# Window scores of all heads in one run and one exponential, split loads of rows, and weights one item later, in an attention and convolution kernel

## The chip, the cores and the metric

The kernel runs on one core of one Trainium2 chip. The metric is the device time of one execution in microseconds (us), as the median of the runs shown. Five engines of the core work side by side, each through its own list of instructions: TensorE (PE, with its weight loads shown as PEld), VectorE (DVE), ScalarE (ACT), GpSimd (POOL) and SyncE (SP), which here only issues transfers. Transfers (DMAs) are issued by SP, ACT or POOL and carried out by 16 shared DMA engines.

## What is computed

The input x has 2 images of 256 channels and 64 x 64 pixels. Two layers follow one another, both in fp32:

```python
# layer 0
q, k, v = 1x1 convolutions of x            # 8 heads of 32 channels, all 4096 pixels
fuse    = softmax(q k^T / sqrt(32)) v
x       = conv1x1(concat(x, fuse)) * m + x * (1 - m)     # m: mask, 32x32 resized to 64x64
# layer 1
x = x * sigmoid(relu(x ca_w1 + ca_b1) ca_w2 + ca_b2)     # gate per pixel and channel
o = softmax(q k^T / 8) v                   # in windows of 8x8 pixels, 4 heads of 64 channels
x = x + o out_w + out_b
x = shuffle(x)                             # channels in 4 groups
y = relu(bn(conv7x7(x, 64 groups)))        # 256 -> 64 channels
y = bn(conv7x7(y, 64 groups))              # 64 -> 256 channels
out = x * sigmoid(y)
```

## The kernel before

**Prologue** (to about 178 us). The 1x1 projections of the 16 chunks (image b, 512 pixels c) are computed (`L450`, `L489`) and stored to DRAM. The copy of v out of PSUM goes through tiles of the tag "v" of a pool with two buffers (`L500`, `L501`); the last chunk's copy is shared by ACT and DVE.

**Attention of layer 0.** For each image b, chunk c, group g of four heads and block m of 128 keys there is a *slot*, 1024 in all. In a slot, `scores` (`L666`) multiplies keys and queries of a block two slots ahead, ACT takes the exponentials (`L679`), `products` (`L718`) multiplies them by v, and DVE adds up the exponentials in two alternating sums (`L724`). In the last chunk there is one sum only (`chains = 1`), so each addition waits for the one before. Denominators (`dn`, `L752`), their reciprocal (`L779`) and the division of the attention result f (`L785`) come some slots later, by a list of due times (`at`). Actions are delayed by a number of slots.

**The stage of a chunk.** `stage(b, c)` (`L789`) is a generator that does the rest of layer 0 and the windows of layer 1 for a finished chunk, while PE goes on with the slots of the next one. One step, up to a `yield`, runs every fourth slot. It computes the mix (hy), the gate (ca1, ca2, tanh), u (`L861`), q and k of the windows in two halves of the heads (`project`, `project_out`), scores, softmax, v, the transposed probabilities (pt, `L980`, `L988`), their product with v (o, `L999`), the output projection (op) and the sum xo = y + u (`L1032`), which is stored to `x_s` in DRAM (`L1047`), padded for the convolutions. The window softmax is done for each half of the heads `hc` separately: 32 matmuls (`L905`), one copy to SBUF (`L913`), one maximum on DVE (`L917`), eight exponentials on ACT with the maximum as bias and the sum as accumulated output (`L926`), then reciprocal and product on DVE (`L937`, `L938`). The stage is put on the list by `at(DN + 8 + late, ...)`; `late` is 5 for most chunks, 13 for the first and 0 for the last two.

**The convolutions.** `convolve()` is a second generator, for the tail. Channels are cut in 16 units u of four input groups. There are 26 *items*: 0 to 8 are units 0 to 8 of image 0, 9 to 15 units 2 to 8 of image 1, 16 to 21 units 9 to 14 with both images (*pair items*), then unit 15 of each image, and units 1 and 0 of image 1. Item k takes its rows from `x_s` (420 KB an image; `load_rows`, `load_x`, on SP), its banded weights from `w_s` (896 KB a unit; `load_w`, `L1088`, on SP), does the first convolution (c1, `L1177`; of pair items `L1144`, which works with differences of columns, `dx`, `L1116`, and sums of weights, `both`, `L1121`, both on DVE), the second (c2, `L1203`), tanh and copy on ACT (`L1214`, `L1220`), the product with x on DVE (`gate`, `L1230`) and 12 or 24 stores of the output (`store`, `L1257`) on several queues. The order within the loop is c1 of item k+1, with `both` of item k+2 behind it, then c2 of k, gate of k, loads of rows, stores of k, and the next weight tile:

```python
conv1(k + 1)
z = conv2(k)
gate(k, z)
load_rows(...)
store(k, z)
if weights and (weights[0] <= 1 + EB or k >= EARLY + 4):
    load_w(weights.popleft())
```

`weights` holds the units 1 to 15 and 1 again; EB is 8 and EARLY is 9. Units 0 to 6 are loaded at the start, 7 to 9 after items 1 to 3, and unit 10 after item 13. As each engine works in the order of the program (the kernel schedules by hand), this order is also that of the queues. Items 0 to 8 begin between the last slots and the last stages. Items of image 1 need the last stage's x_s; the list `staged` says that it has been stored, and then `more()` makes the tiles `xcs` for later items and loads the rows of item 9.

Of the kernel before, what the change touches and what calls it, by code (L numbers as in the profile page):

```python
# [10 lines left out]
F32 = mybir.dt.float32  # L11
# [8 lines left out]
P = 128  # L20
# [37 lines left out]
def conv_seq_kernel(ctx: ExitStack, tc: tile.TileContext, a, out):  # L58
# [315 lines left out]
    with (  # L374
# [109 lines left out]
        for i, (b, c) in enumerate(chunks):  # L484
# [14 lines left out]
            for copy, ms in evict:  # L499
                v = st0.tile([P, KC, 4, P], F32, tag="v", name=f"vst_{b}_{c}_{ms.start}")  # L500
# [55 lines left out]
    def pipeline(arm, shifted, pools):  # L556
# [232 lines left out]
        def stage(b, c):  # L789
# [71 lines left out]
            nc.vector.scalar_tensor_tensor(u, t, 1.0, x1, ALU.add, ALU.mult)  # L861
            yield True

            qks, es_, mxs, sums = [], [], [], []

            def project(hc):
                s = psum2(f"qk{tag}_{hc}")
                for j in range(2):
                    o = (KC * j + hc) * P
                    for kc in range(KC):  # L870
# [25 lines left out]
            def window_scores(hc):  # L896
                qk = qks[hc]
                s = psum2(f"sc{tag}_{hc}")
                for t in range(4):
                    for w in range(2):  # L900
                        for h in range(2):
                            r = slice(64 * h, 64 * h + 64)
                            p = 64 * ((w + t) % 2)
                            tok = slice(t * P + 64 * w, t * P + 64 * w + 64)
                            nc.tensor.matmul(  # L905
                                s[p : p + 64, h, 64 * t : 64 * t + 64],
# [5 lines left out]
                e = wp.tile([P, 8, 64], F32, tag=f"ew{hc}", name=f"ew{tag}_{hc}")  # L912
                nc.scalar.copy(  # L913
                    e.rearrange("p (h n) k -> p h (n k)", h=2), s[:, :, 0 : 4 * 64]
                )
                mx = gp.tile([P, 8], F32, tag=f"mxw{hc}", name=f"mxw{tag}_{hc}")
                nc.vector.tensor_reduce(mx, e, AX.X, ALU.max, negate=True)  # L917
                es_.append(e)
                mxs.append(mx)


            def window_exp(hc):
                e, mx = es_[hc], mxs[hc]
                rs = gp.tile([P, 8], F32, tag=f"rsw{hc}", name=f"rsw{tag}_{hc}")
                for n in range(8):
                    nc.scalar.activation(  # L926
                        e[:, n, :],
                        e[:, n, :],
                        AF.Exp,
                        bias=mx[:, n : n + 1],  # L930
                        accum_out=rs[:, n : n + 1],
                    )
                sums.append(rs)

            def normalise(hc):
                e, rs = es_[hc], sums[hc]
                nc.vector.reciprocal(rs, rs)  # L937
                nc.vector.tensor_mul(e, e, rs.unsqueeze(2).to_broadcast([P, 8, 64]))  # L938
# [520 lines left out]
```

## Time and profile before

| | us |
|---|---|
| runs shown | 2892.77, 2894.96, 2895.96 |
| median | 2894.96 |
| profiled execution | 2891.88 |
| its span | 2890.0 |
| mean granted clock of PE, as a share of full speed | 0.997 |

Of the span, the prologue takes about 178 us, the 1024 slots with the stages of 15 chunks about 2500, and the tail, in which the last stage and the convolutions run, about 210. The heaviest groups of instructions:

```profile
L679 ACT ACTIVATE ea<-sa 128x512 f32<-128x512 f32 (+1 forms) x3072 | 2038.8, 745 | 56.4 <-PE sa L666 24.3
L666 PE MATMUL sa<-qa,ka 32*64 32x512 f32 x16384 | 1145.7, 614 | 3.0 <-DVE vst L501 2.9
L718 PE MATMUL ava<-ea,va 128*32 128x512 f32 x8192 | 1092.0, 605 | 0.4
```

A line of a group names source line, engine, operation, output and inputs with shapes and the count; then busy time in us and the mean of one in ns; then idle time of the engine just before, and what ended most of it. In a timeline a line gives start and length in us, the engine ("SPq" is SP issuing a transfer), the line, what is done, how often in a row, and in brackets how long the engine had been idle and what released it. Matmuls overlap, so what counts of PE is the distance from one start to the next.

### The profile page before, as it was taken

Reading aid. Unit: us, or ns where it says so; the run is one execution under the profiler, and the core shown is the slowest. Engines: PE = TensorE matmul, PEld = TensorE weight load, DVE = VectorE, ACT = ScalarE, POOL = GpSimd, SP = SyncE. Lnnn points to the kernel's source line nnn. Section 1 sums busy time; section 2 is a strip of 40 time slices with the busy share of each in tenths; the row PEclk is TensorE's granted clock in tenths of the full one; section 3 lists DMA queues with packets and bytes.
Section 4 is the critical chain, followed back from the end, with each engine's and each line's share of the span. In section 5 each row is a group of like instructions: output and inputs, shape, how many; then the busy total and the mean of one; then the engine's idle time right before and its main releaser. Section 6 shows DMA issues by size and latency. Waiting matters only on the chain.

```text
span 2890.0 us, 85875 instructions
## 1 busy us (share of the span) xinstructions
PE 2860.5 (99%) x37198; PEld 836.0 (29%) x37198; DVE 2452.6 (85%) x1370; ACT 2459.4 (85%) x4151; POOL 571.0 (20%) x939
## 2 busy tenths in 40 slices
PE   9999999999999999999999999999999999999998
PEld 4541122222222222222222222222222222222676
DVE  3349999999999999999999999999999999999323
ACT  5569989898989898998989898989989898989434
POOL 8111111111111212121120111111211110010376
PEclk9999999999999999999999999999999999999999
DMA  8545433333243434343333334333434432142575
GB/s 262 206 162 189 148 88 74 97 80 91 69 102 77 106 76 95 87 99 87 81 92 75 92 71 96 80 91 84 100 83 89 95 81 84 56 123 64 159 203 137
DMA packets 245755, 305.67 MB, mean 106 GB/s; under 512 B 121272, under 2 KB 137836, under 8 KB 245112
## 3 DMA queue, kind: packets, MB, share of 16 engines
q1 hardware_dynamic: 200084, 231.51, 27.7%
q0 software_dynamic: 40496, 65.79, 12.1%
q8 instruction: 294, 4.82, 0.7%
q10 hardware_dynamic: 4788, 2.79, 0.3%
q14 instruction: 93, 0.76, 0.1%
HBM read 221.88 MB, written 66.39 MB: 100 GB/s over the span
## 4 chain that ended last, share of the span: by engine, by line
PE 94%; DMA 2%; issue 1%; DVE 1%; ACT 1%; SPq 1%; POOL 0%; DVEq 0%; POOLq 0%; ACTq 0%
PE sa L666 36%; PE ava L718 34%; PE hya L552 4%; PE qka L552 4%; PE c2a L1203 2%; PE q L450 2%; PE vwa L552 2%; PE opa L552 2%; PE k L450 2%; PE v L489 2%; PE c1a L1177 1%; PE sca L905 1%; PE c1a L1144 1%; PE oa L999 1%; PE pta L980 1%
## 5 line engine op out<-in xcount | busy, mean ns | idle before, releaser
L679 ACT ACTIVATE ea<-sa 128x512 f32<-128x512 f32 (+1 forms) x3072 | 2038.8, 745 | 56.4 <-PE sa L666 24.3
L666 PE MATMUL sa<-qa,ka 32*64 32x512 f32 x16384 | 1145.7, 614 | 3.0 <-DVE vst L501 2.9
L724 DVE TENSOR_TENSOR suma<-suma,ea 128x2048 f32<-128x2048 f32 x480 | 1096.4, 2284 | 6.2 <-ACT ea L679 1.1
L718 PE MATMUL ava<-ea,va 128*32 128x512 f32 x8192 | 1092.0, 605 | 0.4
L724 DVE TENSOR_TENSOR odda<-odda,ea 128x2048 f32<-128x2048 f32 x420 | 958.3, 2282 | 2.4 <-ACT ea L679 0.5
L696 POOL DMA_DIRECT2D folda<-suma x336 | 235.5, 874 | 1618.4 <-DVE suma L726 1510.3
L666 PEld LDWEIGHTS sa<-qa,ka 32*64 32x64 f32 x16384 | 241.4, 130 | 787.3 <-ACT ea L679 716.7
L718 PEld LDWEIGHTS ava<-ea,va 128*32 128x32 f32 x8192 | 161.6, 108 | 834.0 <-issue 805.2
L1257 POOL DMA_DIRECT2D out_dram<-za x212 | 119.7, 573 | 46.1 <-DVE za L1230 25.6
L552 PE MATMUL qka<-ua,qkv_w 128*32 128x512 f32 x1024 | 115.8, 592 | 0.7 <-DVE ua L861 0.7
L1047 POOL DMA_DIRECT2D xs<-xo x94 | 67.2, 722 | 206.5 <-DVE xo L1032 203.0
L808 ACT ACTIVATE ta<-hya,bf 128x512 f32<-128x512 f32 x32 | 20.2, 684 | 95.2 <-PE hya L552 95.2
L724 DVE TENSOR_TENSOR odda<-ea,ea 128x2048 f32<-128x2048 f32 x30 | 68.6, 2288 | 37.3 <-ACT ea L679 37.3
L469 DVE TENSOR_REDUCE top<-sq 128x128 f32<-128x2048 f32 x16 | 36.6, 2286 | 74.5 <-ACT sq L463 74.5
L764 POOL DMA_DIRECT2D invs<-inva x62 | 34.1, 557 | 287.4 <-DVE inva L779 286.4
L1203 PE MATMUL c2a<-yca,wa 32*64 32x192 f32 (+1 forms) x2912 | 85.0, 368 | 2.2 <-issue 2.0
L926 ACT ACTIVATE ewa<-ewa,mxwa 128x64 f32<-128x64 f32 x256 | 85.3, 346 | 1.5 <-DVE mxwa L917 1.5
L724 DVE TENSOR_TENSOR suma<-ea,ea 128x2048 f32<-128x2048 f32 x32 | 73.2, 2287 | 11.5 <-DMA ka<-ks 8.5
L1214 ACT ACTIVATE za<-c2a 128x384 f32<-128x384 f32 x64 | 27.9, 487 | 62.1 <-PE c2a L1203 34.0
L917 DVE TENSOR_REDUCE mxwa<-ewa 128x8 f32<-128x512 f32 x32 | 21.9, 685 | 63.3 <-ACT ewa L913 63.3
L1203 PEld LDWEIGHTS c2a<-yca,wa 32*64 32x64 f32 x2912 | 67.7, 191 | 18.0 <-issue 10.5
L884 ACT ACTIVATE qka<-qka,qkv_b 128x512 f32<-128x512 f32 x64 | 40.2, 680 | 37.9 <-PE qka L552 37.9
(166 smaller groups left out, 1698.6 us busy)
## 6 DMA issues: line engine op xcount, KB each, us to landing
ka<-ks SPq DMA_DIRECT2D x256, 256.0 KB
va<-vs SPq DMA_DIRECT2D x256, 256.0 KB
wa<-ws SPq DMA_DIRECT2D x17, 896.0 KB
ws<-zeros SPq DMA_DIRECT2D x16, 896.0 KB
folda<-suma POOLq DMA_DIRECT2D x224, 64.0 KB, 3.2
folda<-suma POOLq DMA_DIRECT2D x112, 128.0 KB, 3.6
xs<-xo POOLq DMA_DIRECT2D x78, 140.0 KB, 6.1
qs<-qst SPq DMA_DIRECT2D x16, 512.0 KB
```

Of the source, the lines that this page charges most:

```text
L450: nc.tensor.matmul(s[:, g, :], w[:, kc, g * P : (g + 1) * P], rhs, start=(kc == 0), stop=(kc == KC - 1),)
L489: nc.tensor.matmul(sv[:, m, :], xs0[i][:, kc, m * P : (m + 1) * P], wv[:, kc, :], start=(kc == 0), stop=(kc == KC - 1),)
L552: nc.tensor.matmul(out[o : o + 32], weights[:, o : o + 32], x, start=start, stop=stop)
L666: nc.tensor.matmul(heads[j][o], k[r, cols][:, o], q[r, g, :], start=True, stop=not shifted)
L679: nc.scalar.activation(e[:, h, :], tile, AF.Exp, scale=SCALE0)
L696: nc.gpsimd.dma_start(dst[p : p + rows], total[rows * k : rows * k + rows, h, :], accum_op=ALU.add if k else ALU.bypass,)
L718: nc.tensor.matmul(av[r, :], v[:, m % PB, r], e[:, j, :], start=start, stop=stop)
L724: nc.vector.tensor_add(total, first.pop(m % chains, total), e)
L926: nc.scalar.activation(e[:, n, :], e[:, n, :], AF.Exp, bias=mx[:, n : n + 1], accum_out=rs[:, n : n + 1],)
L1047: eng.dma_start(x_s[b, n, p + r0 : p + r1].rearrange("r g w -> g r w"), xo[64 * h : 64 * h + 64, oc, r0 - WS * c : r1 - WS * c, :],)
L1203: nc.tensor.matmul(tiles[j // 2][o, j % 2, 0 : n * W], w[r, d, o], y[r, 0:n, d : d + W], start=(d == 0), stop=(d == KS - 1),)
L1257: eng.dma_start(*args)
```

## The change

The window softmax of a stage is done for all heads at once: both projections, then one run of 64 score matmuls into one PSUM tile, one copy, one maximum, a subtraction on DVE, one exponential of 128x1024 on ACT without bias and without accumulated sum, and sum, reciprocal and product on DVE. A stage has two steps fewer. u is made in two halves and `project` goes over its inputs in the outer loop. The tag "v" gets three buffers. The stage of chunk (1,6) starts four slots later. The last stage stores its x_s in three parts of the channels and, after the first, loads the rows of items 9 to 11. Rows are loaded up to item k+4; while item k has one image, they are loaded in three pieces an image, put between the stores of item k on SP (`queue`). c1 of odd items with one image uses another PSUM tile. Copy and gate of the last two items go by blocks of rows, and their stores and those of the two items before go by other queues. `both` and `yt` use other SBUF tiles. Weight units 10 to 15 and 1 are issued from item 14 on (`EARLY + 5`).

```diff
-                v = st0.tile([P, KC, 4, P], F32, tag="v", name=f"vst_{b}_{c}_{ms.start}")
+                v = st0.tile([P, KC, 4, P], F32, tag="v", name=f"vst_{b}_{c}_{ms.start}", bufs=3)
...
-            nc.vector.scalar_tensor_tensor(u, t, 1.0, x1, ALU.add, ALU.mult)
+            for oc in range(KC):
+                nc.vector.scalar_tensor_tensor(
+                    u[:, oc], t[:, oc], 1.0, x1[:, oc], ALU.add, ALU.mult
+                )
             yield True
 
-            qks, es_, mxs, sums = [], [], [], []
+            qks = []
...
-                for j in range(2):
-                    o = (KC * j + hc) * P
-                    for kc in range(KC):
+                for kc in range(KC):
+                    for j in range(2):
+                        o = (KC * j + hc) * P
...
-            def window_scores(hc):
-                qk = qks[hc]
-                s = psum2(f"sc{tag}_{hc}")
+            project_out(0, project(0))
+            yield True
+            project_out(1, project(1))
+            yield True
+            s = psum2(f"sc{tag}")
+            for hc, qk in enumerate(qks):
...
+                            at0 = 64 * (4 * hc + t)
-                                s[p : p + 64, h, 64 * t : 64 * t + 64],
+                                s[p : p + 64, h, at0 : at0 + 64],
...
-                e = wp.tile([P, 8, 64], F32, tag=f"ew{hc}", name=f"ew{tag}_{hc}")
-                nc.scalar.copy(
-                    e.rearrange("p (h n) k -> p h (n k)", h=2), s[:, :, 0 : 4 * 64]
-                )
-                mx = gp.tile([P, 8], F32, tag=f"mxw{hc}", name=f"mxw{tag}_{hc}")
-                nc.vector.tensor_reduce(mx, e, AX.X, ALU.max, negate=True)
-                es_.append(e)
-                mxs.append(mx)
...
-                    nc.scalar.activation(
-                        e[:, n, :],
-                        e[:, n, :],
-                        AF.Exp,
-                        bias=mx[:, n : n + 1],
-                        accum_out=rs[:, n : n + 1],
-                    )
-                sums.append(rs)
...
-            def normalise(hc):
-                e, rs = es_[hc], sums[hc]
-                nc.vector.reciprocal(rs, rs)
-                nc.vector.tensor_mul(e, e, rs.unsqueeze(2).to_broadcast([P, 8, 64]))
-
-            project_out(0, project(0))
+            e = wp.tile([P, 16, 64], F32, tag="ew", name=f"ew{tag}")
+            nc.scalar.copy(e.rearrange("p (h n) k -> p h (n k)", h=2), s)
+            mx = gp.tile([P, 16], F32, tag="mxw", name=f"mxw{tag}")
+            nc.vector.tensor_reduce(mx, e, AX.X, ALU.max)
+            nc.vector.tensor_sub(e, e, mx.unsqueeze(2).to_broadcast([P, 16, 64]))
             yield True
-            window_scores(0)
-            yield
-
-            s = project(1)
-            window_exp(0)
-            project_out(1, s)
-            yield True
-            window_scores(1)
-            normalise(0)
-            yield
...
-            window_exp(1)
+            nc.scalar.activation(e, e, AF.Exp)
             nc.scalar.copy(v, sv)
+            rs = gp.tile([P, 16], F32, tag="rsw", name=f"rsw{tag}")
+            nc.vector.tensor_reduce(rs, e, AX.X, ALU.add)
+            nc.vector.reciprocal(rs, rs)
+            nc.vector.tensor_mul(e, e, rs.unsqueeze(2).to_broadcast([P, 16, 64]))
             yield True
-            normalise(1)
-            yield
...
-                                    es_[hc][p : p + 64, 4 * h + 2 * tt + odd, :],
+                                    e[p : p + 64, 8 * h + 4 * hc + 2 * tt + odd, :],
...
-            ots = []
+            ots = wp.tile([P, KC, CH], F32, tag="ew", name=f"ot{tag}")
             for kc in range(KC):
-                ot = wp.tile([P, CH], F32, tag=f"ew{kc}", name=f"ot{tag}_{kc}")
-                ots.append(ot)
...
-                for n, (x0, _, _) in enumerate(BLOCKS):
-
-                    r0, r1 = max(WS * c, x0 - 1), min(WS * c + WS, x0 + 31)
...
+            last = (b, c) == (B - 1, NCHUNK - 1)
+            parts = [(UG * 2, UG * 5), (UG * 5, NG), (0, UG * 2)] if last else [(0, NG)]
+            for g0, g1 in parts:
+                for oc in range(KC):
+                    for n, (x0, _, _) in enumerate(BLOCKS):
+                        r0, r1 = max(WS * c, x0 - 1), min(WS * c + WS, x0 + 31)
+                        if r0 >= r1:
+                            continue
+                        for h in range(2):
+                            q = 2 * oc + h
+                            p = 32 * q + 1 - x0
+                            eng = nc.sync if h == 1 and last else nc.gpsimd
+                            eng.dma_start(
+                                x_s[b, n, p + r0 : p + r1, g0:g1].rearrange("r g w -> g r w"),
+                                xo[64 * h + g0 : 64 * h + g1, oc, r0 - WS * c : r1 - WS * c, :],
+                            )
+                if last and g0 == UG * 2:
+                    staged[0](EARLY + 2)
...
-            def load_x(k):
+            def load_x(k, queue=None):
                 u, images = items[k]
                 x = xs[k] = early[k % 4] if k < EARLY else xcs[(k - EARLY) % len(xcs)]
                 for i, b in enumerate(images):
-                    nc.sync.dma_start(
-                        x[:, nb * i : nb * i + nb].rearrange("p n g w -> p n (g w)"),
-                        x_s[b, :, :, UG * u : UG * u + UG, :].rearrange("n p g w -> p n (g w)"),
-                    )
-
-            def load_rows(k):
+                    to = x[:, nb * i : nb * i + nb].rearrange("p n g w -> p n (g w)")
+                    src = x_s[b, :, :, UG * u : UG * u + UG, :].rearrange("n p g w -> p n (g w)")
+                    if queue is None:
+                        nc.sync.dma_start(to, src)
+                    else:
+                        queue.extend((to[:, n], src[:, n]) for n in range(nb))
+
+            def load_rows(k, queue=None):
 
                 while len(xs) < min(k + 1, len(items)) and (
-                    staged or B - 1 not in items[len(xs)][1]
+                    xcs or B - 1 not in items[len(xs)][1]
                 ):
-                    load_x(len(xs))
+                    load_x(len(xs), queue)
...
-                both = wp.tile([P, 8, 64], F32, tag="ew0", name=f"both{arm}{k}")
+                both = wp.tile([P, 2, CH], F32, tag="qk0", name=f"both{arm}{k}")
...
-                t = wp.tile([P, CH], F32, tag="ew1", name=f"yt{arm}{k}")[:, 0 : n * W]
+                t = wp.tile([P, 2, CH], F32, tag="qk1", name=f"yt{arm}{k}")
+                t = t.rearrange("p n k -> p (n k)")[:, 0 : n * W]
...
-                s = psum1(f"c1{arm}{k}")
+                if k % 2:
+                    s = avp.tile([P, CH], F32, tag="av", name=f"c1{arm}{k}")
+                else:
+                    s = psum1(f"c1{arm}{k}")
...
+            def blocks_of(k, t):
+                if k < len(items) - 2:
+                    return [t]
+                return [t[:, :, n] for n in range(nb)]
...
-                    nc.scalar.activation(z, z, AF.Copy, bias=0.25, scale=0.25)
-                    zs.append(z.rearrange("p j (n x) -> p j n x", x=W))
+                    z = z.rearrange("p j (n x) -> p j n x", x=W)
+                    for part in blocks_of(k, z):
+                        nc.scalar.activation(part, part, AF.Copy, bias=0.25, scale=0.25)
+                    zs.append(z)
...
-                    nc.vector.tensor_mul(zs[m], zs[m], x.rearrange("p n g x -> p g n x"))
-
-            def store(k, zs):
+                    x = x.rearrange("p n g x -> p g n x")
+                    for z_, x_ in zip(blocks_of(k, zs[m]), blocks_of(k, x)):
+                        nc.vector.tensor_mul(z_, z_, x_)
+            def store(k, zs, queue):
                 u, images = items[k]
...
                 elif k == len(items) - 2:
-                    engines = (nc.scalar, nc.sync, nc.sync)
-                elif k == len(items) - 3:
-                    engines = (nc.gpsimd, nc.sync, nc.sync)
-                elif len(images) == 2:
+                    engines = (nc.sync, nc.scalar, nc.sync, nc.gpsimd)
+                elif k >= len(items) - 4 or len(images) == 2:
                     engines = (nc.gpsimd, nc.sync)
+                each = -(-3 * len(queue) // (nb * 4))
...
+                            for _ in range(each if eng is nc.sync else 0):
+                                if queue:
+                                    nc.sync.dma_start(*queue.popleft())
                             if eng is nc.scalar:
                                 held.append(lambda a=args: nc.scalar.dma_start(*a))
                             else:
                                 eng.dma_start(*args)
+                while queue:
+                    nc.sync.dma_start(*queue.popleft())
...
-            def more():
-                if staged and not xcs:
-
+            def last_rows(k):
+                if not xcs:
...
-                    load_rows(EARLY)
-                return bool(xcs)
+                load_rows(k)
+
+            staged.append(last_rows)
...
-                    if not more():
+                    if not xcs:
                         yield
+                    else:
+                        load_rows(len(xs))
...
-                more()
                 z = conv2(k)
                 yield
-                more()
...
+                queue = deque()
                 if xcs:
-                    load_rows(min(len(xs) + (k >= EARLY - 1), k + len(xcs)))
+                    load_rows(k + 4, queue if len(images) == 1 else None)
                 elif k + 4 < EARLY:
-                    load_rows(k + 4)
+                    load_rows(k + 4, queue)
                 if k == 1:
-                    store(0, first)
-                store(k, z)
-                if weights and (weights[0] <= 1 + EB or k >= EARLY + 4):
+                    store(0, first, deque())
+                store(k, z, queue)
+                if weights and (weights[0] <= 1 + EB or k >= EARLY + 5):
                     load_w(weights.popleft())
...
                 late = 5 if (b, c) < (B - 1, NCHUNK - 2) else 0
                 if (b, c) == (0, 0):
                     late = EB + 5
+                elif (b, c) == (B - 1, NCHUNK - 2):
+                    late = 4
                 at(DN + 8 + late, lambda b=b, c=c: stages.append(stage(b, c)))
...
-        staged.append(True)
```

## The prediction

> **What bounds the kernel now.** I read the page first, then the table of stretches, then the start and the tail as timelines, the chain, the waits and the costliest groups. The page's busy line says whose time it is:
>
> ```profile
> PE 2860.5 (99%) x37198; PEld 836.0 (29%) x37198; DVE 2452.6 (85%) x1370; ACT 2459.4 (85%) x4151; POOL 571.0 (20%) x939
> ```
>
> TensorE (PE) is busy 99% of the span, so only what shortens PE's own work, or opens or closes one of its gaps, moves the end. A middle chunk and a piece of the tail, as rows of the table of stretches (length; then busy time of PE, PEld, DVE, ACT, POOL; granted clock, DMA share, GB/s):
>
> ```profile
> 992.00:1149.00 157.00, 156.98 (x2000) 37.35 (x1996) 146.25 (x77) 142.80 (x245) 26.87 (x40) 1.00 0.38 89
> ```
> ```profile
> 2797.00:2845.00 48.00, 46.35 (x1062) 36.55 (x1062) 23.09 (x29) 20.26 (x39) 31.50 (x56) 1.00 0.74 221
> ```
>
> In the chunk PE has no gap; VectorE (DVE) is idle for 157.00 - 146.25 = 10.8 us, ScalarE (ACT) for 14.2. In the tail PE is still nearly full, but DMA engines are 74% busy: there the weights come in time or not. The timeline of SP's queue, DVE and PE there:
>
> ```profile
> 2818.89 7.71 SPq L1257 DMA_DIRECT2D out_dram<-za  x12
> 2826.69 0.35 SPq L1088 DMA_DIRECT2D wa<-ws  x1
> ...
> 2831.86 0.57 DVE L1121 TENSOR_TENSOR botha<-wa 128x384 f32<-128x384 f32 x1 [0.60 <-DMA wa<-ws]
> ...
> 2836.57 0.35 SPq L1088 DMA_DIRECT2D wa<-ws  x1
> 2837.76 7.03 SPq L1257 DMA_DIRECT2D out_dram<-za  x12
> 2841.29 0.59 DVE L1121 TENSOR_TENSOR botha<-wa 128x384 f32<-128x384 f32 x1 [1.02 <-DMA wa<-ws]
> 2842.42 1.35 PE L1144 MATMUL c1a<-xla,botha 128*32 128x192 f32 x24
> ```
>
> The reader should see three things: the weight tile is issued only behind the 12 stores before it; `both` waits for it already (0.60 and 1.02 us); and PE's next convolution starts 0.5 us after `both` ends. A weight tile has no time left to lose.
>
> **The change, part by part.** All sums are made against the profiled execution: 2891.88 us, of which the span is 2890.0 and 1.88 lies around it. The median of the runs shown is 2894.96, so 3.1 is added at the end.
>
> *Prologue: a third buffer for the v copy.* DVE's last copy of v starts at 176.67 because it waits for a store to release its buffer, and the first score matmul waits 2.92 us for it. ACT's copy in the same eviction starts at 174.88. With a free buffer DVE starts there as well: **-1.8 us**.
>
> *Window attention.* Scores move from two runs of 32 matmuls to one of 64:
>
> ```profile
> L905 PE MATMUL sca<-qka 64*64 64x64 f32 x1024 | 22.2, 224 | 0.4 <-ACT qka L884 0.4
> L980 PE MATMUL pta<-ident,ewa 64*64 64x64 f32 x1024 | 18.6, 221 | 0.0
> L926 ACT ACTIVATE ewa<-ewa,mxwa 128x64 f32<-128x64 f32 x256 | 85.3, 346 | 1.5 <-DVE mxwa L917 1.5
> L917 DVE TENSOR_REDUCE mxwa<-ewa 128x8 f32<-128x512 f32 x32 | 21.9, 685 | 63.3 <-ACT ewa L913 63.3
> L938 DVE TENSOR_TENSOR ewa<-ewa,rswa 128x512 f32<-128x512 f32 x32 | 22.2, 692 | 3.3 <-DVE rswa L937 0.5
> L861 DVE SCALAR_TENSOR_TENSOR ua<-sga,x1a 128x1024 f32<-128x1024 f32 x16 | 19.5, 1218 | 6.0 <-ACT sga L852 6.0
> L988 ACT COPY pta<-pta 128x1024 f32<-128x1024 f32 x16 | 16.2, 1013 | 2.3 <-PE pta L980 1.6
> ```
>
> A run of 32 takes 0.62 us to PE's next work, twice per chunk; the transposes are one run of 64 of the same shape and take 1.09. So 0.15 per chunk, 15 chunks: **-2.2 us**. ACT loses 16 exponentials (starts about 0.33 apart, 5.3 us) and two half copies (0.61 each) and gains one exponential and one copy of 128x1024, each like the copy to pt at 1.01: -4.5 us a chunk. That is the change's name, yet it is worth nothing: ACT was idle 14.2 us of the chunk and PE waited for nothing there. [...]
>
> DVE pays. Per chunk two maxima (0.69), two reciprocals (0.23) and two products (0.69) go; a maximum, a subtraction, a sum and a product over 1024 columns come, at 1.22 by the widest row above or twice 0.69 = 1.38, less the pipeline part they share; on starts to the next instruction I count 1.13 each, plus one reciprocal. u in two halves costs 0.07. Sum: 6.0 against 4.1, **+1.9 us of DVE per chunk**. In the middle it hides in DVE's 10.8 idle us: 0. If that cover were gone it would cost 15 x 1.9 = 28 us.
>
> *Last chunk.* There it isn't covered:
>
> ```profile
> 2648.61 35.83 DVE L724 TENSOR_TENSOR suma<-suma,ea 128x2048 f32<-128x2048 f32 x15
> ```
>
> That is 2.39 per addition without a pause. PE gains more here: the stage of chunk (1,6) starts four slots later, which takes away a wait of 0.94 for its f, and c1 of odd items takes another PSUM tile, which takes away 0.87 before c1 of item 1. So PE is 1.8 + 2.2 + 0.9 + 0.9 = 5.9 us ahead, ready for the denominators at 2680.1, before 2685.96. DVE comes in 4.0 earlier, but has 1.9 more to do for the stage, and xo (1.2, at 2698.16 in before) now falls ahead of its last additions: 0.9 earlier, 2683.5 in place of 2684.44. **PE keeps 2.4 of the 5.9**; 3.4 become a wait for DVE.
>
> *Between attention and the convolutions.* u in halves lets PE start its projections 0.76 earlier; 0.45 of waiting goes with the second run of scores, 0.46 at c1 of item 5 (psum), 0.15 with the joined run: -1.8. Then the row loads. The x_s stores of the last stage go out in three parts of the channels and item 9's rows are loaded behind the first. Before, PE waited 2.69 at c1 of item 9 (2759.30). The page's DMA issues and the chain show what for:
>
> ```profile
> xs<-xo POOLq DMA_DIRECT2D x78, 140.0 KB, 6.1
> ```
> ```profile
> 2755.55 3.62 DMA xla<-xs
> 2759.16 0.14 issue
> 2759.30 2.54 PE c1a L1177 x53
> ```
>
> xo ends at 2748.57, POOL has issued the x_s stores by 2749.69, 6.1 later they have landed, and the load goes out at 2755.55: 10.7 from xo to c1. After, the first part has 12 of 64 channels; I bound its landing by the 24 KB stores of the output (4.8) and the shortest landing in the chain (2.1): issue 0.7 to 1.4, landing, load 3.1 to 3.8 come to 5.9 to 10.0. But by PE's instruction order c1 of item 7 (2.5) now comes before the projection that feeds xo, not after it. So the wait becomes 2.7 + 2.5 - (0.7 to 4.8) = 0.4 to 4.5; I take 2.2, the middle: -0.5. Item 4's third row piece stands behind a store on SP: +0.3 (0 to 0.6). The rows come as three pieces; I take their load as unchanged, within the 3.1 to 3.8. [...] Items 9 to 15 stand 5.04 apart, but three of these steps took 6.02, 5.27 and 6.18: 2.4 us of short waits, of which I take half as gone with the second PSUM tile (0 to 2.4). So at the end of c2 of item 14, before at 2796.98, PE is 2.4 + 1.8 + 0.5 - 0.3 + 1.2 = **5.6 us earlier (3.5 to 8.0)**. Call this moment t = 0.
>
> *Weights one item later.* `load_w` for tiles 10 to 15 and the second 1 now waits for k >= 14, not 13: each is issued behind the stores of one later item. In the order of SP's instructions w10 stands behind item 14's stores, w11 behind item 15's, up to w15 behind item 19's. Tile w(10+j) is needed by `both` of item 17+j, and that stands on DVE ahead of the gate of item 15+j, whose product the next stores write, behind which the next weight is queued. PE's c1(17+j) begins with the `both` terms, so PE stops too. So a loop closes: `both` 0.57, first gate 0.96, 12 stores on SP (7.0 to 9.9 in before, against a load of weights running beside them; at least 0.42 each = 5.0), weight issue 0.35, landing 4.3 to 5.0 (issued 2826.69, `both` 2831.86; issued 2836.57, `both` 2841.29; issued 2844.89, landed 2849.33). That is 11.2 to 14.4 us per item, where PE needs c1 4.14 + c2 4.80 = 8.94 (c1 of items 20 and 21 at 2833.43 and 2842.42).
>
> Counted from t = 0: c1 of 17 at 11.9 to 13.8 (before 2804.87 - 2796.98 = 7.89), of 18 some 9.9 later, of 19 another 12.2 to 13.3 behind twelve stores, then 11.7 to 13.9 for each of 20 and 21 and 11.0 to 13.2 for 22, the first without `both`. c1 of 22 at 68.5 to 78 where it was 2851.35 - 2796.98 = 54.4: **+14 to +23.5; I take +17**, nearer to the low end: by SP's instruction list each transfer waits for the eighth before it, so in before the sixth store of a burst waited for the weight's landing, and after, the weight has landed when the stores go. If PE had cover for one item of delay, this would be 0.
>
> *End.* Gate and copy of the last two items in blocks, one held ACT store fewer (0.6 each) and other queues: **-0.8** (0 to -1.5). The remaining c1 and c2 are unchanged; w1 for item 24 has 5.03 us of landing and the same PE work ahead of it: 0.
>
> Sum: -5.6 + 17 - 0.8 = **+10.6** (from -8.0 + 14 - 1.5 = +4.5 to -3.5 + 23.5 = +20). On the profiled execution 2891.88 + 10.6 = 2902.5; on the median 2894.96 + 10.6 = **2905.5**.
>
> **Rivals.**
> 1. *The late weights are hidden* (faster). If SP gets to the weight early enough that issue to `both` fits in the 8.94 us of a pair item, nothing is lost: -5.6 - 0.8 = -6.4, 2888.5. It decides from twelve stores in under 8.94 - 0.57 - 0.96 - 0.35 - 4.65 = 2.4 us, where the fastest burst in this region took 7.03. Against it: `both` waits already. For it: the trace has no burst without a weight load ahead of it, so how fast one can be is unseen. Chance 0.10.
> 2. *No measurable change.* Loop at its low end (+14, or fewer items caught in it) and the gains at their high end (-9.5): +4.5 or less, 2899. Chance 0.12.
> 3. *SP is worse than I count.* For items 12 to 15 SP now carries 6 row pieces and 4 stores per item of 5.0 us; at 0.42 each that fits, but not with the wait for the eighth before: bursts of 12 took up to 9.9. Then w10 and w11 slip too: +20 to +29 net, 2915 to 2924. Chance 0.10.
> 4. *DVE becomes the bound in the middle.* Idle 10.8 against +1.9: it would need DVE to be late at one particular slot in every chunk, 1 to 2 us x 15 = 15 to 28 more, 2919 to 2932. Chance 0.03.
>
> **Numbers.** Forecast 0.65, rivals as given. Differences within 0.2% (5.8 us) are about what a measurement of this kernel can't tell from no change. Faster 0.10; same 0.12 plus the low tail of the forecast 0.02 = 0.14; slower 0.76. Range: the forecast's +4.5 to +20 is 2899.5 to 2915; to leave out no more than 2 in 10 it reaches down to 2896, into rival 2.
>
> **What will show it.** Right: `both` waits 3 to 7 us for the weights in each of five or six items, and PE has gaps of the same size between 2795 and 2865; c1 of pair items starts 11 to 14 us apart; the denominators wait for DVE; one ACT exponential of about 1.05 us per chunk; PE's middle chunks shorter by 0.15 only. Wrong: pair items still 8.94 apart (rival 1), or PE gaps inside the middle chunks (rival 4), or long SP bursts already at items 12 to 15 (rival 3).

## The result, and the profile after

The changed kernel takes 2907.9 us (median; 2901.97 to 2910.81), the kernel before, timed beside it, 2895.28 (2892.66 to 2896.23). The ratio is 1.0044, 95% interval 1.0031 to 1.0057: slower by about 12.6 us. The forecast was 2905.5. The profiled execution is one of the two longest, 2910.76, with a span of 2908.7: 18.7 more than the span before.

The page's busy line, and the rows of the table of stretches for the same middle chunk and the same piece of the tail as before:

```profile
PE 2860.3 (98%) x37198; PEld 834.7 (29%) x37198; DVE 2485.0 (85%) x1374; ACT 2393.7 (82%) x3643; POOL 576.1 (20%) x946
```
```profile
992.00:1149.00 157.00, 156.98 (x2004) 37.18 (x2000) 148.62 (x78) 139.40 (x212) 27.00 (x40) 1.00 0.38 89
2797.00:2845.00 48.00, 33.78 (x717) 24.31 (x712) 15.84 (x19) 13.05 (x25) 20.30 (x37) 0.86 0.62 184
```

PE is busy for as long as before to 0.2 us (slower matmuls behind some waits, below, are in that), so the 18.7 shows as idle time of PE. In the middle chunk PE still has no gap; DVE is busy for 2.4 us more there and ACT for 3.4 less. These two rows count what falls between fixed times, after the change one DVE instruction more (78, 77), so the page's totals are the better measure: over 16 stages DVE has 32.4 us more, about 2.0 a stage, and ACT 65.7 less, about 4.1 a stage. In the tail PE worked 33.8 of 48 us where it had worked 46.4, and DMA engines were less busy than before (a share of 0.62, before 0.74): nobody is overloaded, everybody waits for somebody. The timeline of SP's queue, DVE and PE there shows for whom:

```profile
2833.23 5.51 SPq L1247 DMA_DIRECT2D out_dram<-za  x12
2838.84 0.35 SPq L1061 DMA_DIRECT2D wa<-ws  x1
...
2845.53 0.56 DVE L1096 TENSOR_TENSOR botha<-wa 128x384 f32<-128x384 f32 x1 [4.51 <-DMA wa<-ws]
2846.41 1.83 DVE L1218 TENSOR_TENSOR za<-za,xla 128x768 f32<-128x768 f32 x2 [0.31 <-ACT za L1198]
2847.40 5.06 SPq L1247 DMA_DIRECT2D out_dram<-za  x12
2852.56 0.35 SPq L1061 DMA_DIRECT2D wa<-ws  x1
...
2858.40 0.56 DVE L1096 TENSOR_TENSOR botha<-wa 128x384 f32<-128x384 f32 x1 [5.74 <-DMA wa<-ws]
2859.07 2.16 PE L1119 MATMUL c1a<-xla,botha 128*32 128x192 f32 x24 [3.85 <-ACT za L1206]
```

This is the loop: `both` ends at 2846.09, the gate follows at 2846.41, the twelve stores at 2847.40, the weight at 2852.56, the next `both` at 2858.40. From one `both` to the next it is 12.87 us (0.9 to the gate, 1.0 to the stores, 5.2 for them, 5.8 for the weight), where PE has 8.94 of work. The last line names ACT as the releaser, but what came last was `both`, which ended at 2858.96, 0.1 before c1. In all DVE waited 26.3 us for weights, in five items (the list of waits of the tail: "DVE botha L1096 <- DMA wa<-ws: 26.3, 5, 8.3": total, times, longest).

Where the 18.7 us lie, by the starts of c1 on PE:

| stretch | before | after | difference |
|---|---|---|---|
| start to the end of c2 of item 14 | 2796.98 | 2791.65 | -5.3 |
| from there to c1 of item 22 | 54.4 | 80.3 | +25.9 |
| c1 of item 22 to the end of the span | 38.65 | 36.7 | -1.95 |

### The profile page after: what moved, and what is told of

It reads as the page before. It is cut to its first block, busy times and chain, and to the rows that moved or that the text cites. A ratio compares the mean times of both kernels' runs of the same rounds, so it can differ in the third digit from the quotient of the medians.

```text
span 2908.7 us, 85482 instructions
## 1 busy us (share of the span) xinstructions
PE 2860.3 (98%) x37198; PEld 834.7 (29%) x37198; DVE 2485.0 (85%) x1374; ACT 2393.7 (82%) x3643; POOL 576.1 (20%) x946
## 4 chain that ended last, share of the span: by engine, by line
PE 88%; DMA 3%; DVE 3%; issue 2%; SPq 1%; POOL 1%; ACT 1%; DVEq 0%; ACTq 0%; POOLq 0%
PE sa L666 35%; PE ava L718 33%; PE hya L552 4%; PE qka L552 4%; PE v L489 2%; DVE suma L724 2%; PE vwa L552 2%; PE k L450 2%; PE opa L552 2%; PE q L450 1%; POOL out_dram L1247 1%; SPq L1247 1%; PE sca L912 1%; PE ca2a L843 1%; DMA wa<-ws 1%
## 5 line engine op out<-in xcount | busy, mean ns | idle before, releaser
L724 DVE TENSOR_TENSOR odda<-odda,ea 128x2048 f32<-128x2048 f32 x420 | 957.9, 2281 | 33.8 <-ACT ea L679 33.8
L726 DVE TENSOR_TENSOR suma<-suma,odda 128x2048 f32<-128x2048 f32 x30 | 68.8, 2292 | 1.0
L724 DVE TENSOR_TENSOR odda<-ea,ea 128x2048 f32<-128x2048 f32 x30 | 68.5, 2284 | 1.2 <-ACT ea L679 1.2
L812 DVE TENSOR_TENSOR ta<-ta,mca 128x512 f32<-128x512 f32 x32 | 22.0, 688 | 43.5 <-ACT ta L808 43.5
```

What stands on the lines that cost most here:

```text
L724: nc.vector.tensor_add(total, first.pop(m % chains, total), e)
L726: nc.vector.tensor_add(acc[1], acc[1], acc[2])
```

## The experiments

All of these kernels were timed against the kernel before; ratios come with their 95% intervals. Times and distances within a kernel are read from single profiled executions. The waits of `both` for the weights in e1, e2 and e3, in this order (total, times, longest):

```profile
DVE botha L1096 <- DMA wa<-ws: 2.8, 1, 2.8
DVE botha L1121 <- DMA wa<-ws: 23.5, 5, 6.1
DVE botha L1096 <- DMA wa<-ws: 6.1, 3, 3.1
```

**e1: the later weights undone.**

```diff
-                if weights and (weights[0] <= 1 + EB or k >= EARLY + 5):
+                if weights and (weights[0] <= 1 + EB or k >= EARLY + 4):
```

> The changed kernel with one thing undone: weight units 10 to 15 and 1 are issued from item 13 on again (EARLY + 4). My theory: the whole loss is the loop of both, gate, twelve stores and weight that the later issue closes; without it the rest of the change gains what the changed kernel's trace shows ahead of item 16 (5.3 us) and at the end (1.9 us): 2895.3 - 7 = 2888 (2885 to 2890), and c1 of pair items is about 9 us apart. Rival A, the row loads in pieces between the stores crowd SP whatever the weights do: 2895 to 2905, with waits of both for the weights remaining. Rival B, the softmax on DVE costs in the tail or in the chunks: 2893 or more.

Measured: 2885.49 against 2893.88, ratio 0.9965 (0.9953 to 0.9977). c1 of items 18 to 20 stood 8.96 and 9.00 apart, `both` waited once (2.8 us, for w14). So the rest of the change gains about 8 to 10 us, and the one line loses the ratio from 0.9965 to 1.0044, about 23 us (21 by a second measurement of e1, below), since the ratios are 0.0079 and 0.0072 apart. Rivals A and B fall.

**e2: the later weights alone, in the kernel before.**

```diff
-                if weights and (weights[0] <= 1 + EB or k >= EARLY + 4):
+                if weights and (weights[0] <= 1 + EB or k >= EARLY + 5):
```

> The kernel before with one thing of the change alone: weight units 10 to 15 and 1 are issued from item 14 on (EARLY + 5), one item later each. My theory: all of the loss comes with it, so 2895.3 + 17 to 26 = 2912 to 2921, both waits 4 to 8 us for the weights in most pair items, and c1 of pair items is 11 to 16 us apart. Rival A (the pieces of rows on SP are needed for the loss): under 2903, both hardly waits more than before.

Measured: 2920.24 against 2893.88, ratio 1.0095 (1.0080 to 1.0111), 26 us more. `both` waited 23.5 us in five items and pair items were 11.8 to 14.7 apart. The loss needs nothing else of the change: here, too, the bursts of twelve stores were short, 5.2 to 5.9 us, and the weight behind them took 4.7 to 7.5.

**e3: as late as in the change, but ahead of the stores.**

```diff
+                if weights and k >= EARLY + 5:
+                    load_w(weights.popleft())
                 store(k, z, queue)
-                if weights and (weights[0] <= 1 + EB or k >= EARLY + 5):
+                if k < EARLY + 5 and weights[0] <= 1 + EB:
                     load_w(weights.popleft())
```

> The changed kernel, weights still from item 14 on, but each issued ahead of the stores of its item instead of behind them. It tells whether the item counts or the twelve stores on SP's queue. My theory: the stores are the link that closes the loop, so this is nearly the earlier issue again: 2888 (2886 to 2892), c1 of pair items about 9 to 9.5 us apart. Rival C, one item of delay is too much by itself, wherever the issue stands in the item (landing too short before both): 2898 or more, both still waiting 3 us or more in each item.

Measured: 2885.74 against 2893.88, ratio 0.9975 (0.9966 to 0.9984). Pair items stood 9.0 apart, but for 10.4 and 10.5 at two of the waits; `both` waited 1.6, 1.5 and 3.1 us at items 17, 20 and 21. Its ratio can't be told from e1's, and rival C falls: what costs is not the item of delay but the twelve stores, with the gate that they wait for, ahead of the weight on SP.

**e4 and e4b: TensorE kept busy in the waits.** 48 matmuls, then 24, of a tile of zeros ahead of c1 of items 17 to 21, into the PSUM tile that c1 overwrites:

```diff
                 s = psum1(f"c1{arm}{k}")
+                for f in range(FILL if k > EARLY + 7 else 0):
+                    r = 32 * (f % 4)
+                    nc.tensor.matmul(
+                        s[r : r + 32, 0 : 2 * c], ident[:, 0:32], keep, start=True, stop=True
+                    )
```

> The changed kernel with 48 idle matmuls of a tile of zeros, about 4 us, put on TensorE ahead of c1 of items 17 and later pair items, into the PSUM tile that c1 then overwrites; no other work is changed. After waits of 3.9 to 6.6 us the profile shows a granted clock of 0.54 to 0.65 and c1 takes 5.9 to 6.6 us instead of 4.1. Theory: the clock falls after TensorE has idled over some 3 us, and keeping it busy avoids that: c1 takes 4.1 in all of these items, granted clock 1.00 there, and the time falls by 1 to 3 us (2905 to 2907), as only c1 of item 17 is on the loop. Rival D, the clock has nothing to do with the idling (it is drawn by something else there): c1 stays at 5.9 and the time rises by up to 4 us per item that isn't waiting, 2908 to 2920.

> The filler again at half the count, 24 matmuls, as 48 took 7.8 us and not 4: about 3.9 us ahead of c1 of the pair items 17 to 21, less than or about as long as the waits of 6.1, 0.1, 6.6, 2.6 and 3.9 us that the changed kernel has there. Theory: granted clock near 1.00 and c1 of 4.1 us in these items as with 48, and, since the loop through gate, stores and weight sets the time, at most 1 to 3 us less than the changed kernel (2905 to 2908). Rival D2: also this filler lengthens the loop, 2910 or more.

Measured with 48: 2920.81, ratio 1.0093 (1.0077 to 1.0108). I had set the size wrong: 48 such matmuls take 7.8 us, not 4. Items then stood 16.7 apart, which is 7.8 + 8.94, with no wait on PE: here PE was the bound, and the time went up. With 24 (3.9 us): 2907.53, ratio 1.0036 (1.0023 to 1.0049), not to be told from the changed kernel's 1.0044. Two things can be read from it. First, items stood 12.72, 12.88, 12.79, 12.83 and 12.86 apart, as in the changed kernel's last steps (13.79, 12.87, 12.92): PE got 3.9 us more work in each and these steps did not grow, so the loop sets them, not PE. Second, the clock. The timelines of PE, the changed kernel first, then e4b, at c1 of item 17 and at the end of the 24 matmuls:

```profile
2805.91 2.16 PE L1119 MATMUL c1a<-xla,botha 128*32 128x192 f32 x24 [6.14 <-DVE botha L1096]
2807.82 0.89 PE L1119 MATMUL c1a<-xla,wa 128*32 128x192 f32 x8
2808.46 2.38 PE L1119 MATMUL c1a<-dxa,wa 128*32 128x192 f32 x32
2810.66 1.25 PE L1119 MATMUL c1oa<-dxa,wa 128*32 128x192 f32 x24
```
```profile
2801.00 4.08 PE L1112 MATMUL c1a<-keep,ident 128*32 128x384 f32 x48
2806.96 1.38 PE L1127 MATMUL c1a<-xla,botha 128*32 128x192 f32 x24 [1.88 <-DVE botha L1099]
2808.10 0.58 PE L1127 MATMUL c1a<-xla,wa 128*32 128x192 f32 x8
2808.48 1.62 PE L1127 MATMUL c1a<-dxa,wa 128*32 128x192 f32 x32
2809.91 1.30 PE L1127 MATMUL c1oa<-dxa,wa 128*32 128x192 f32 x24
```

(The profile counts two for each fp32 matmul of the filler: x48 for 24.) After 6.1 us of waiting the same 24 matmuls take 2.16 and not 1.38, and it takes some 4.8 us until they are back at speed.

**e5: the window softmax alone, in the kernel before.** The steps of the stage from the score run to the product with v as in the change, with the tiles that they need; u, `project`, rows, stores and weights as before.

```diff
-            window_scores(0)
-            yield
...
+            nc.vector.tensor_sub(e, e, mx.unsqueeze(2).to_broadcast([P, 16, 64]))
...
+            nc.scalar.activation(e, e, AF.Exp)
```

> The kernel before with the window softmax of the change alone (one run of scores, one tile, one exponential, subtraction on DVE, two steps fewer in a stage); weights, rows, stores and the v copy as before. My theory: ACT's saving of some 4.5 us a chunk is worth nothing, the joined run of scores shortens a chunk by 0.23 as in the changed kernel's trace (157.24 in place of 157.47), 14 to 15 times, so about 3 us less until the last chunk, of which DVE's longer work there may take back some: 2893.9 - 1 to -3.5 = 2890.5 to 2893. Rival E, the softmax itself is what gains in the changed kernel (ACT was a bound): 2886 or less. Rival F, DVE's added 1.9 us a chunk costs: chunks of 158 or more, 2897 or more.

Measured: 2893.98 against 2895.35, ratio 0.9998 (0.9989 to 1.0007): nothing. The trace shows why. Chunks last 157.24 and not 157.47 from one mix to the next, 2.8 us in twelve; but the last distance, from the mix of chunk (1,6) to that of (1,7), is 139.55 and not 136.34. Two lines of its timeline show where they go, DVE's wait ahead of the maximum (0.66 in before) and PE's wait at the denominators (none in before):

```profile
2613.45 1.22 DVE L919 TENSOR_REDUCE mxwa<-ewa 128x16 f32<-128x1024 f32 x1 [2.41 <-ACT ewa L917]
2683.83 1.93 PE L752 MATMUL dna<-suma,keysum 128*32 128x128 f32 x32 [3.01 <-DVE suma L724]
```

In the last chunk DVE is the bound, and every additional us there, and the wait for ACT's copy of the scores, delays its last addition. The denominators behind PE's wait are slow, too: 1.93 us, where the same 32 matmuls take 1.08 in the changed kernel. The name of the change is worth nothing by itself.

**e6: no pieces.** e1, with the rows loaded whole ahead of the stores.

```diff
-                    load_rows(k + 4, queue if len(images) == 1 else None)
+                    load_rows(k + 4)
                 elif k + 4 < EARLY:
-                    load_rows(k + 4, queue)
+                    load_rows(k + 4)
```

> The changed kernel with the weights from item 13 on (EARLY + 4) and without the pieces: the rows of a later item are loaded whole, ahead of the stores of the item, as in the kernel before. Theory: the pieces are worth little either way, since PE's steps of 5.04 us at items 9 to 15 leave the loads time: 2884 to 2888, beside 2885.5 with the pieces. Rival G, the pieces bring part of the gain (short stores no longer stand behind a whole load): 2889 or more. Rival H, each piece pays a fixed time, so that whole loads are better: 2883 or less.

Measured: 2885.24 against 2895.35, ratio 0.9967 (0.9955 to 0.9978). The pieces neither gain nor cost what can be measured.

**e7, and e1 and e7 again: a better version?** e7 has the weights from item 13 on and ahead of the stores, and 16 matmuls of zeros ahead of c1 of item 9, where PE waits for rows.

```diff
+                for f in range(16 if k == EARLY else 0):
+                    r = 32 * (f % 4)
+                    nc.tensor.matmul(
+                        s[r : r + 32, 0:384], ident[:, 0:32], keep, start=True, stop=True
+                    )
...
+                if weights and k >= EARLY + 4:
+                    load_w(weights.popleft())
                 store(k, z, queue)
-                if weights and (weights[0] <= 1 + EB or k >= EARLY + 5):
+                if k < EARLY + 4 and weights[0] <= 1 + EB:
                     load_w(weights.popleft())
```

> The changed kernel with the weights from item 13 on and each ahead of the stores of its item, and 16 idle matmuls of zeros (2.6 us) ahead of c1 of item 9, where PE waits 2.9 us for rows and c1 and c2 then ran slowly (4.2 in place of 2.5). Theory: the wait for w14 (2.8 on DVE, 1.3 on PE) goes, and c1 of item 9 takes 2.5: 2885.5 - 1.3 - 1.7 = 2882.5 (2880 to 2885), faster than both kernels. Rival: the filler delays c1 by as much as it saves, and the weights meet the loads of rows: 2886 or more.

> The changed kernel with the weights from item 13 on, a second time. The variants without the later stage of (1,6) and without the split of x_s came out at ratios of 0.998, this kernel at 0.9965 in another job, a difference of 5 us where the traces show 2. If those traces are the whole of it, this kernel comes out at 0.9970 to 0.9980 now, 2886.5 to 2889; if the two parts are worth 5 us each, at 0.9965 or less again.

> The kernel with weights from item 13 on and ahead of the stores, and idle matmuls ahead of c1 of item 9, a second time, beside the kernel that it builds on. Its trace shows c1 of item 9 at 2.5 us and pair items 9.0 apart without a wait. Theory: 2 to 4 us less than its neighbour. Rival: no difference beyond 1 us, the time goes elsewhere (the end, where the last stores go out).

Measured: e7 2885.57, ratio 0.9966 (0.9953 to 0.9979); in a later measurement e1 2885.15, 0.9972 (0.9962 to 0.9982), and e7 2885.14, 0.9969 (0.9960 to 0.9978). e7 does what it was made for: c1 of item 9 takes 2.5 us, in neither of its two traces does a `both` wait for a weight, and pair items stand 9.0 to 9.4 apart. Yet it gains nothing over e1. From c1 of item 22 to that of 25 e7 needs 19.8 and 20.1 us in its two traces, e1 18.4 and 17.9, and ACT waits 14.1 and 14.0 us there for stores of the output to free its z tiles, in e1 8.0 and 7.3: what was won ahead is given back where the last stores go out. So e1, the change without its later weights, is as good as any of these, and beats both kernels by 0.3% (before) and 0.75% (after).

**e8: e1 with the stage of (1,6) not delayed.**

```diff
-                elif (b, c) == (B - 1, NCHUNK - 2):
-                    late = 4
```

> The changed kernel with the weights from item 13 on, and the stage of chunk (1,6) as early as in the kernel before (not four slots later). Theory: the wait of 0.94 for its f returns on PE, but at the denominators of the last chunk PE waits 2.5 us for DVE anyway, so the wait there shrinks by as much and the time stays: 2884 to 2888, beside 2885.5. Rival I, the four slots are worth their wait: 2887 to 2889, the denominators at the same distance behind DVE. Rival J: the later stage delays DVE's last additions, so that without it the time falls, 2883 or less.

Measured: 2890.15 against 2895.4, ratio 0.9983 (0.9974 to 0.9992). My theory fell; rival I has nearly the size, but not the mechanism, as PE's wait for DVE is not the same. From the denominators (dn) of chunk (1,6) to c1 of item 2 this trace needs 154.6 us, those of e1 (its first trace) and e9, which have the delay, 151.6. The two timelines of DVE, e8 first and then e9, at the maximum in the last chunk:

```profile
2610.05 1.22 DVE L922 TENSOR_REDUCE mxwa<-ewa 128x16 f32<-128x1024 f32 x1 [2.34 <-ACT ewa L920]
```
```profile
2617.08 1.22 DVE L922 TENSOR_REDUCE mxwa<-ewa 128x16 f32<-128x1024 f32 x1 [0.91 <-ACT ewa L920]
```

Four slots later DVE idles 0.91 and not 2.34 ahead of the maximum; 1.4 us of its bound chunk are saved there, and PE's wait at dn is 2.45 and not 3.85. After the 3.85 the second half of dn also takes 1.79 and not 1.08, and the c2 behind it 3.50 and not 2.64, slow matmuls behind a wait again.

**e9: e1 with the x_s stores of the last stage whole.**

```diff
-            parts = [(UG * 2, UG * 5), (UG * 5, NG), (0, UG * 2)] if last else [(0, NG)]
+            parts = [(0, NG)]
...
-                if last and g0 == UG * 2:
+                if last:
```

> The changed kernel with the weights from item 13 on, and the x_s stores of the last stage whole, with the rows of items 9 to 11 loaded behind all of them. Theory: the split by channels shortens the way from xo to c1 of item 9 by about 1 to 2 us, since the first part lands 3.6 us after its issue where the whole took about 6; PE's wait for rows grows from 2.9 to 4 to 5: 2886.5 to 2888. Rival K, the split is worth nothing (the landing time does not depend on the size): 2884 to 2886, the wait as before.

Measured: 2888.93 against 2895.4, ratio 0.9985 (0.9976 to 0.9995). PE's wait at c1 of item 9 is 4.02 us (e1: 2.89 and 2.47 in its two traces) and c1 then takes 4.71 (4.19 and 2.54): 1.7 more than in the first trace and 3.7 more than in the second, as the theory has it. The medians of e8 and e9 stand 4.8 and 3.6 above that of e1 (2885.3 in the mean of its two measurements), the traces show 3.0 and 1.7 to 3.7. The two ratios of e1 (0.9965 and 0.9972) differ by 2 us, about as much as the rest, so the rest stays open; that both parts gain a little is shown by the traces, and by the medians in sign. The third buffer of "v", u in halves, the second PSUM tile and the new end were not taken out one by one: what they are worth is read from traces alone.

## Why the prediction was right, step by step

The forecast, the sign and the mechanism held: the front gains, and the loop through `both`, gate, stores and weight takes more than it gains. The rivals did not come about. That the median came out only 2 us above the forecast is in part luck: the execution that was profiled lost 18.7, and one term was mis-sized by 9 in it.

- *v copy.* Predicted -1.8, measured -1.1: the first score matmul starts at 176.64 (177.72), after a wait of 1.75 and not 2.92. DVE's copy started at 175.59, when ACT's had just ended, and not beside it at 174.97.
- *Joined scores.* Predicted 0.15 a chunk, measured 0.23. ACT's saving is 4.1 us a stage by the page's totals, predicted 4.5, and worth nothing, as predicted. The exponential took 1.07 (1068 ns in the mean of 16), the forecast said 1.01 by the nearest row, and about 1.05 in its list of signs, a value that none of its rows gives.
- *DVE.* Predicted +1.9 a chunk, measured +2.0 by the page's totals (2485.0 - 2452.6 over 16 stages); the four operations take 1.21 to 1.23 each. It hides in the middle, as predicted.
- *Last chunk.* PE waited 2.45 for DVE at the denominators; the forecast was 3.4. The four slots of delay work through DVE and ACT's copy (e8), not only through the 0.94 of PE that I named. The c2 behind the denominators started 4.1 earlier than before (2683.77, 2687.84), forecast 2.4, but then took 4.23 in place of 2.64, at a granted clock of 0.58 (2683.8 to 2687.9): 1.6 us that no step had. That 2.5 were left at the next c1 (2687.93, 2690.41), as forecast, is luck.
- *Rows of item 9.* Wait 3.06, forecast 2.2 (0.4 to 4.5). Landing of the first part 3.58, load 4.64, over the 3.8 that I allowed. What no step had: c1 behind the wait took 3.57 and c2 3.17, where 2.54 and 2.64 are usual, 1.5 us more, at granted clocks of 0.69 and 0.80.
- *All up to item 14.* Forecast -5.6, measured -5.3, in part by luck: the two slow stretches above cost 3.1, and from c1 of item 2 until PE waits for item 9's rows it gained 3.0 (66.2 us, now 63.2), forecast 1.8.
- *Weights.* **This term was mis-sized**: I took +17 of a range of 14 to 23.5, and the profiled execution shows +25.9. c1 of items 17 to 22 came at 14.3, 25.1, 40.8, 54.6, 67.4 and 80.3 from t = 0, forecast 11.9 to 13.8 for the first and 68.5 to 78 for the last. The way to item 17 and the steps to 18 and 19 (14.3, 10.9, 15.6) lie above their forecasts (up to 13.8, 9.9, up to 13.3), those to 20, 21 and 22 (13.8, 12.9, 12.9) within theirs. The bursts of stores were fast, as argued: 5.06 to 5.51 in items 17 to 20, 7.05 in item 16. The trace of before shows what stretched them there: in two bursts the seventh store (the prediction says the sixth), eighth behind the weight, started at 2831.83 and 2841.26, 0.03 ahead of the `both` of that weight. But a weight took 5.0 to 6.9 us from its issue to its use (2811.12 to 2816.10, 2838.84 to 2845.53, 2865.07 to 2871.99), where I had allowed 4.65 to 5.35 (0.35 for the issue and 4.3 to 5.0); in e2 it took 4.7 to 7.5. Why, the traces don't settle: a load of rows follows 0.4 to 0.5 us behind it, but in before it followed as closely, 0.5 to 0.7; that the twelve stores ahead of it are now issued in 5 us and not in 7, and are still on their way, is only argued. And c1 ran slowly after three of the waits, by 1.8 to 2.5 us each, of which that of item 17 lies on the loop, and 0.3 of that of item 19 (the gate at 2846.41 waited for ACT). Part of the miss is the execution: by the medians the kernel lost 12.6 and not 18.7, which with the other two terms as they are leaves about 20 for this one.
- *End.* Forecast -0.8, measured -1.95.
- *Sums that don't come out.* The loop's upper end, 14.4, leaves no room for the burst of 9.9 that stands in the same sentence; with it the sum is 16.8. The middle of 0.4 to 4.5 is 2.45, not 2.2. The bounds of the terms up to item 14 add up to 1.8 to 8.9 earlier, not 3.5 to 8.0, and 1.8 + 2.2 + 0.94 + 0.87 is 5.8, not 5.9. The 6.1 us of landing is the page's median over all chunks; counted from 2749.69 it ends at 2755.79, after the load had gone out at 2755.55. None of these moves the forecast by more than 0.3 us; the first makes the range too narrow above.

The sum in the profiled execution is -5.3 + 25.9 - 1.95 = +18.7, forecast +10.6; by the medians it is +12.6. The gains were right to 1.2 us; the loop was found and priced too low in it.

## What to carry to other kernels

A transfer's place in the queue is more than a time: behind stores that wait for a product which waits, on another engine, for the transfer before, it closes a loop, and then each round pays the sum of all links (12.87 us here, with 8.94 of work for PE). Before moving an issue "one item later", write down what stands ahead of it in its queue and what that waits for; e3 shows that the same delay ahead of the stores costs nothing that can be measured. And a saving on an engine that isn't the bound (ACT here) is only as good as the price on the engine that becomes the bound somewhere (DVE in the last chunk): e5 came out at 0.9998.

## What the runs showed of the hardware

A wait of PE can cost more than its length. The rows of the changed kernel's table of stretches (length; PE, PEld, DVE, ACT, POOL busy; granted clock, DMA share, GB/s) after waits of 6.1, 6.6 and 3.9 us, and of e4b's, where the filler ran:

```profile
2806.00:2812.00 6.00, 6.00 (x96) 4.27 (x104) 1.05 (x3) 0.32 (x1) 4.54 (x8) 0.65 0.52 139
2832.00:2838.00 6.00, 5.59 (x76) 3.98 (x80) 2.08 (x3) 0.25 (x1) 4.50 (x8) 0.54 0.45 110
2859.00:2866.00 7.00, 6.93 (x96) 4.79 (x104) 2.35 (x4) 0.32 (x1) 5.82 (x11) 0.59 0.36 68
```
```profile
2829.00:2842.00 13.00, 13.00 (x256) 8.51 (x252) 5.05 (x6) 4.44 (x9) 6.75 (x12) 1.00 0.67 190
2842.00:2855.00 13.00, 13.00 (x256) 8.23 (x252) 4.97 (x6) 4.40 (x10) 6.75 (x12) 1.00 0.35 80
```

The granted clock was 0.54 to 0.65 for some 5 us after such a wait, and 1.00 where idle matmuls filled it, although they multiply zeros. The length of the wait alone does not decide it: c1 of item 9 took 2.54 after waits of 2.69 (before) and 2.68 (e6), but 4.19 after 2.70 (e3) and 2.89 (e1), and c1 of item 17 was slow in part after 1.90 (e3: 1.83 for its first 24 matmuls, where 1.35 is usual). So the "some 3 us" of e4's theory is no limit here, and what else decides it these traces don't show.
